# Routing a mixture of experts back to its tokens: row scatters in place of row gathers in a decoder block on one core

## The chip, the cores and the metric

The kernel runs on one core of a Trainium2 chip. The metric is the device time of one execution in microseconds (us). The engines are TensorE (PE in profiles; its weight loads are PEld), VectorE (DVE), ScalarE (ACT), GpSimd (POOL) and SyncE (SP, which here only issues transfers). Each works through its own queue in order; they meet at semaphores. Transfers (DMAs) issued by SP and ACT, and those issued by GpSimd, share sixteen DMA engines.

## The reference

One decoder block on x of 8 sequences x 256 tokens x 256 features, all in float32. Three steps, each followed by a LayerNorm over the sum with its input: causal self-attention with 16 heads; three rounds of slot attention over a context of 120 rows with a GRU cell; and a mixture of experts. The last step is where the change lies:

```python
router_probs = softmax(x @ gate_w + gate_b)              # 8 experts
expert_values, expert_indices = top_k(router_probs, k=2)
expert_values = expert_values / (sum(expert_values) + 1e-09)
all_outputs = gelu(x @ ew1[e] + eb1[e]) @ ew2[e] + eb2[e]  # 256 -> 1024 -> 256
moe_out = sum over the two chosen experts of value * output
return x + mlp(x, shared weights) + moe_out
```

Only the two chosen experts of a token matter to its result.

## The kernel before

There are NT = 2048 tokens in NBLK = 4 blocks of 512; a block is four groups of 128 tokens, a token to a partition. `X[i]` holds block i with tokens on the partitions, `XT[i]` the same with features on the partitions.

Attention comes first, then the slot attention as twelve phases (three rounds of four blocks). At the start of the second stage `zeros` fills two tables in DRAM through SP: `xd` and `yd`, each 16,640 rows of 256 numbers. A table has a region of 2048 rows for each expert, and a tail of rows that stay zero.

Routing of block i: `route_rest(i)` makes the probabilities, the two one-hot choices `hot1` and `hot2` and the weights `wt1` and `wt2`. In `best`, `first` is the rank (8 for expert 0, down to 1 for expert 7) of the chosen expert. `place(i)` counts, for each token, which row of its expert's region it gets, and writes the row numbers into `slots[0]` and `slots[1]`. Then GpSimd scatters the block to `xd`: eight indirect DMAs (line 892), four groups times two choices, 128 rows each. The 32 scatters of all blocks are declared independent of one another (`declare_no_dep`), so that none waits for another's landing. place(0) comes in the last phase of the second stage, place(1), (2) and (3) between units of the shared MLP.

`tables()` works out, from the counts of each expert, which expert and which rows each of the 23 tiles gets: 16 pair tiles of 256 rows and 7 single tiles of 128 rows, enough for every possible routing. Rows that no token filled are zero. SP reads the tile's expert and first row into registers (`tei`, `tri`).

For each tile: `tile_fetch` loads its rows of `xd` (line 1114), waiting by hand-written dependencies for all 32 scatters; `tile_weights` and `tile_weights2` load the expert's weights (2 MB a tile); `tile_turn` transposes the rows on TensorE (line 1147); `tile_up` (line 1044, `ph_t`) and `tile_down` (line 1058, `pf_t`) are the two matrix products with gelu on ScalarE between them (line 1053). `tile_down` adds the bias into `yo` and stores it through SP to the tile's rows of `yd` (line 1162). The tiles are pipelined: the up product of a tile comes ahead of the down product of the one before.

The shared MLP is cut into eight units u of 256 tokens with the same two products (`ph_s`, `pf_s`). Units 0 to 3 come before the tiles, among the routing; units 4 to 7 come after them, in the tail. `Z[i]` collects the result of block i.

The tail: `fetch_back(i)` gathers, for each group and choice, the 128 rows of `yd` by `slots` with an indirect DMA of GpSimd (line 1172), 32 in all, into 16 buffers `y`. `take_back(i)` adds them to `Z[i]` with their weights (line 1186, eight VectorE operations a block). `finish` applies the LayerNorm and stores the output (line 1190). The order is written out:

```python
    shared_up(4)
    fetch_back(0)
    shared_up(5)
    fetch_back(1)
    take_back(0)
    parts(4)
    take_back(1)
    shared_up(6)
    ...
    for i in range(2):
        finish(i, 0, NSUB)
    fetch_back(2)
```

The order on TensorE and ScalarE is that of the program throughout; in the tail also that on VectorE and GpSimd. Everything else, SP always among it, is put in order by the planner of the framework, which also inserts the semaphores. It knows a dependency through DRAM only by the table: an indirect access may touch any row of it.

Of the kernel before, what the change touches and what calls it, by code (L numbers as in the profile page):

```python
# [18 lines left out]
NT = B * S  # L19
# [27 lines left out]

SHARED_FIRST = 4

NY = 16  # L50
LN_EPS = 1e-5
RMS_EPS = 1e-6
ATT_EPS = 1e-6
# [8 lines left out]
def decoder_kernel(  # L62
# [44 lines left out]
            nc.scalar.copy(dst, src)  # L107


    X = [act.tile([P, NSUB, D], F32, tag=f"X{i}", name=f"X{i}") for i in range(NBLK)]  # L110
    XT = [act.tile([P, DC, BLK], F32, tag=f"XT{i}", name=f"XT{i}") for i in range(NBLK)]

    def load_x(i):
# [407 lines left out]
    b2p = stage2.enter_context(tc.tile_pool(name="b2", bufs=2))  # L521

    shared = load_shared()
    zeros = b1.tile([P, D], F32, name="zeros")
# [288 lines left out]
    def route_rest(i):  # L813

        shape = [P, NSUB, NE]

        def t(name):
            return fr2.tile(shape, F32, tag=name, name=f"{name}_{i}")

        def s(name):  # L820
            return fr2.tile([P, NSUB], F32, tag=name, name=f"{name}_{i}")

        def wide(a):
            return a.unsqueeze(2).to_broadcast(shape)
# [17 lines left out]
        def best(src, k, hot):  # L842
            top, first = s(f"top{k}"), s(f"first{k}")
# [11 lines left out]
        top2 = best(rest, 2, hot2[:, blk, :])  # L855
# [11 lines left out]
    puts = []  # L867

    def place(i):

        blk = ts(i, NSUB)
        shape = [P, NSUB, NE]
        pc = bank(f"place_{i}")[:, 0 : NSUB * NE]
        flat = [a[:, blk, :].rearrange("p n e -> p (n e)") for a in (cur, before)]
        nc.tensor.matmul(pc, upper, flat[0], start=True, stop=False)
        nc.tensor.matmul(pc, ones, flat[1], start=False, stop=True)
        row = fr2.tile(shape, F32, tag="row", name=f"row_{i}")
        tt(
            row,
            pc.rearrange("p (n e) -> p n e", e=NE),  # L880
            first_row[:, 0:NE].unsqueeze(1).to_broadcast(shape),
            ALU.add,
        )
        for j, hot in enumerate((hot1, hot2)):
            tt(hot[:, blk, :], hot[:, blk, :], row, ALU.mult)
            at_row = fr2.tile([P, NSUB], F32, tag=f"at_row{j}", name=f"at_row{j}_{i}")
            nc.vector.tensor_reduce(at_row, hot[:, blk, :], AX.X, ALU.add)
            nc.vector.tensor_copy(slots[j][:, blk], at_row)
        for n in range(NSUB):
            for slot in slots:  # L890
                g = i * NSUB + n
                put = nc.gpsimd.indirect_dma_start(
                    out=xd[:, :],
                    out_offset=bass.IndirectOffsetOnAxis(ap=slot[:, g : g + 1], axis=0),
                    in_=X[i][:, n, :],
                    in_offset=None,
                )
                if puts:
                    tc.declare_no_dep(put.ins, group="puts", reason="other rows")
                tc.add_to_no_dep_group("puts", put.ins)  # L900
                puts.append(put)

    def tables():

# [194 lines left out]
        tt(z, z, po, ALU.add)  # L1099
        yield  # L1100

    TI = {}

    def groups(t):
        return 2 if t < NPAIRT else 1
# [4 lines left out]
    def tile_fetch(t):  # L1110

        row = nc.sync.value_load(tri[0:1, t : t + 1], min_val=0, max_val=ROWS - RT)
        xg = f2.tile([P, 2, D], F32, tag="xg", name=f"xg_{t}", bufs=4)[:, 0 : groups(t), :]
        load = nc.sync.dma_start(xg, rows_of(xd, row, t))
        for put in puts:
            tc.add_manual_dep(
                load.ins,
                put.ins.name,
                mybir.DependencyInfo(mybir.DependencyClass.Sync, mybir.DependencyReason.DATA),
                reason="rows of the table",  # L1120
            )
        TI[t] = [row, xg]

    def tile_weights(t):

# [7 lines left out]
        TI[t] += [w1_sb, w2_sb, bt, b2t, e]  # L1133

    def tile_weights2(t):

        row, xgT, w1_sb, w2_sb, bt, b2t, e = TI[t]
        nc.sync.dma_start(w2_sb, ew2[ds(e, 1), :, :].rearrange("e (c p) d -> p (e c) d", p=P))
        nc.sync.dma_start(b2t, b2[ds(e, 1), :].to_broadcast([P, D]))

    def tile_turn(t):
# [8 lines left out]
        TI[t][1] = xgT  # L1150

    def tile_up(t):
        row, xgT, w1_sb, w2_sb, bt, b2t, e = TI[t]
        HT["t", t] = up(w1_sb, bt, xgT, f"t{t}")

    def tile_down(t):
        row, xgT, w1_sb, w2_sb, bt, b2t, e = TI.pop(t)
        n = groups(t)
        po = down(w2_sb, HT.pop(("t", t)), f"t{t}", groups=n)
        yo = f2.tile([P, 2, D], F32, tag="yo", name=f"yo_{t}")[:, 0:n, :]  # L1160
        tt(yo, po[:, 0:n, :], b2t.unsqueeze(1).to_broadcast([P, n, D]), ALU.add)
        nc.sync.dma_start(rows_of(yd, row, t), yo)

    Y = {}

    def fetch_back(i):

        for n in range(NSUB):
            for j, slot in enumerate(slots):
                g = i * NSUB + n  # L1170
                y = f2.tile([P, D], F32, tag="y", name=f"y_{g}_{j}", bufs=NY)
                nc.gpsimd.indirect_dma_start(  # L1172
                    out=y,
                    out_offset=None,
                    in_=yd[:, :],
                    in_offset=bass.IndirectOffsetOnAxis(ap=slot[:, g : g + 1], axis=0),
                )
                Y[g, j] = y

    def take_back(i):  # L1180

        for n in range(NSUB):
            g = i * NSUB + n
            for j, wt in enumerate((wt1, wt2)):
                z = Z[i][:, n, :]
                nc.vector.scalar_tensor_tensor(z, Y.pop((g, j)), wt[:, g : g + 1], z, ALU.mult, ALU.add)  # L1186

    def finish(i, n0, n1):
        layernorm(Z[i][:, n0:n1, :])
# [154 lines left out]
```

## Time and profile before

| | |
|---|---|
| median of 9 runs | 1095.49 us (1094.92 to 1097.65) |
| the profiled execution | 1097.89 us, of which the span of instructions is 1096.2 |
| TensorE busy | 1040.5 us, 95% of the span |
| ScalarE, VectorE, GpSimd busy | 475.5, 469.6, 237.6 us |
| mean granted TensorE clock | 0.982 of full speed |
| moved by DMA | 144.24 MB, mean 132 GB/s |
| GpSimd's gathers, line 1172 | 32, 946 ns median each |
| GpSimd's scatters, line 892 | 32, 960 ns median each |
| expert weights | 46 loads of 1 MB, 5.6 us to landing (median) |

A row of a timeline or of the chain gives the start in us from the span's beginning, the duration in us, the engine, the line of the kernel, the operation, what it writes and reads, and how often. In brackets stands how long the engine had been idle and whose event ended that. "issue" is time in which an engine waited for nothing that the profile shows; "remote" or "an unknown queue" is a wait whose releaser the profile can't name. "SPq" is SP's own queue of instructions. A row of stretches gives, for each engine, busy us and the number of instructions in it, the granted clock, the share of time that the DMA engines were busy, and GB/s.

### The profile page before, as it was taken

Reading aid. Unit: us, or ns where it says so; the run is one execution under the profiler, and the core shown is the slowest. Engines: PE = TensorE matmul, PEld = TensorE weight load, DVE = VectorE, ACT = ScalarE, POOL = GpSimd, SP = SyncE. Lnnn points to the kernel's source line nnn. Section 1 sums busy time; section 2 is a strip of 40 time slices with the busy share of each in tenths; the row PEclk is TensorE's granted clock in tenths of the full one; section 3 lists DMA queues with packets and bytes.
Section 4 is the critical chain, followed back from the end, with each engine's and each line's share of the span. In section 5 each row is a group of like instructions: output and inputs, shape, how many; then the busy total and the mean of one; then the engine's idle time right before and its main releaser. Section 6 shows DMA issues by size and latency. Waiting matters only on the chain. (4 is left out here: it accounts for less than half of the span.)

```text
span 1096.2 us, 13674 instructions
## 1 busy us (share of the span) xinstructions
PE 1040.5 (95%) x4686; PEld 720.4 (66%) x4686; DVE 469.6 (43%) x1394; ACT 475.5 (43%) x1140; POOL 237.6 (22%) x264
## 2 busy tenths in 40 slices
PE   8999999999888999999999999699999999999867
PEld 4444555555445755555565668588888888888756
DVE  3666666666676542434443677400011011110137
ACT  3567776666676024555555443123222222222213
POOL 2333423532234221121211023500000000000550
PEclk9999999999999999999999998999999999999969
DMA  9644433333344499940000011246676767663231
GB/s 326 105 78 82 87 70 61 73 73 72 70 90 89 150 348 348 349 145 0 1 1 1 0 39 39 78 154 219 205 243 208 232 202 250 213 211 110 84 92 64
DMA packets 195492, 144.24 MB, mean 132 GB/s; under 512 B 107551, under 2 KB 185951, under 8 KB 195423
## 3 DMA queue, kind: packets, MB, share of 16 engines
q1 hardware_dynamic: 191263, 132.88, 42.7%
q0 software_dynamic: 3072, 8.39, 2.4%
q10 hardware_dynamic: 1088, 2.10, 0.5%
q8 instruction: 37, 0.61, 0.2%
q14 instruction: 32, 0.26, 0.1%
HBM read 72.70 MB, written 45.48 MB: 108 GB/s over the span
## 5 line engine op out<-in xcount | busy, mean ns | idle before, releaser
L1053 ACT ACTIVATE hT_t<-ph_t,bt 128x256 f32<-128x256 f32 (+1 forms) x184 | 71.1, 437 | 202.7 <-issue 154.6
L363 POOL TENSOR_TENSOR sc<-sc,sums 128x256 f32<-128x256 f32 (+1 forms) x128 | 105.2, 843 | 213.2 <-DVE sums L360 213.2
L348 ACT ACTIVATE sc<-sc,nmax 128x128 f32<-128x128 f32 (+1 forms) x256 | 113.3, 444 | 73.8 <-DVE nmax L335 73.8
L1044 PE MATMUL ph_t<-xgT,w 128*128 128x256 f32 (+1 forms) x736 | 140.3, 348 | 0.8 <-ACT hT_t L1053 0.8
L1058 PE MATMUL pf_t<-w,hT_t 128*128 128x256 f32 x624 | 138.3, 379 | 0.0
L739 PE MATMUL gate<-XT,whh_sb 128*128 128x512 f32 x288 | 133.8, 593 | 0.0
L1044 PEld LDWEIGHTS ph_t<-xgT,w 128*128 128x128 f32 x736 | 123.8, 190 | 15.0 <-ACT hT_t L1053 1.0
L1058 PEld LDWEIGHTS pf_t<-w,hT_t 128*128 128x128 f32 x624 | 116.9, 190 | 15.0
L1172 POOL DMA_INDIRECT y<-yd,slot x32 | 30.7, 959 | 323.8 <-PE ph_s L1044 309.2
L335 DVE CUSTOM_DVE_ANT_0 sc<-pp,mask 128x128 f32<-128x128 f32 (+1 forms) x256 | 76.3, 354 | 54.2 <-PE pp L323 53.3
L377 ACT COPY planes<-sc 128x1536 uint16<-128x1536 uint16 x64 | 93.2, 1457 | 8.5 <-POOL sc L363 8.5
L1044 PE MATMUL ph_s<-XT,sh 128*128 128x256 f32 x256 | 66.5, 415 | 20.8 <-issue 11.3
L739 PEld LDWEIGHTS gate<-XT,whh_sb 128*128 128x128 f32 x288 | 54.2, 189 | 48.5 <-issue 46.2
L399 PEld LDWEIGHTS po<-pT,v 128*64 128x64 f32 x512 | 33.2, 137 | 68.3 <-issue 25.5
L1044 PEld LDWEIGHTS ph_s<-XT,sh 128*128 128x128 f32 x256 | 52.9, 209 | 33.0 <-issue 14.6
L399 PE MATMUL po<-pT,v 128*64 128x256 f32 (+1 forms) x512 | 56.4, 340 | 19.1 <-DVE pT L385 13.9
L748 PEld LDWEIGHTS gate<-at,G 120*128 120x128 f32 x288 | 54.5, 189 | 29.9 <-issue 23.3
L748 PE MATMUL gate<-at,G 120*128 120x256 f32 x288 | 72.1, 379 | 0.4 <-DVE at L598 0.4
L1149 DVE COPY xgT<-xg 128x512 f32<-128x512 f32 (+1 forms) x23 | 14.0, 610 | 131.7 <-PE xg L1147 131.7
L385 DVE COPY pT<-turned 128x1536 uint16<-128x1536 uint16 x64 | 69.3, 1082 | 0.0
L598 DVE TENSOR_TENSOR yo<-pf_t,b2t 128x512 f32<-128x512 f32 (+1 forms) x23 | 14.0, 611 | 127.9 <-PE pf_t L1058 127.9
L1053 ACT ACTIVATE hT_s<-ph_s,vec_sb 128x256 f32<-128x256 f32 x64 | 26.7, 470 | 90.5 <-PE ph_s L1044 45.5
(208 smaller groups left out, 1479.9 us busy)
## 6 DMA issues: line engine op xcount, KB each, us to landing
w<-in_ew_dram SPq DMA_DIRECT2D x46, 1024.0 KB, 5.6
xd<-zeros SPq DMA_DIRECT2D x1, 16640.0 KB, 51.2
yd<-zeros SPq DMA_DIRECT2D x1, 16640.0 KB, 99.4
xg<-xd SPq DMA_DIRECT2D x16, 256.0 KB, 5.4
yd<-yo SPq DMA_DIRECT2D x16, 256.0 KB, 5.7
b2t<-in_b_dram SPq DMA_DIRECT2D x23, 128.0 KB, 5.4
sh<-in_sh_w_dram SPq DMA_DIRECT2D x2, 1024.0 KB, 6.9
X<-in_x_dram SPq DMA_DIRECT2D x3, 512.0 KB, 11.6
```

The source lines that it names most:

```text
L335: nc.vector.tensor_tensor_reduce(out=sc[:, h, seg[t]], in0=pp[h][:, seg[t]], in1=mask[:, seg[t]], scale=-(HD**-0.5), scalar=3.0e38, op0=AL ...
L348: nc.scalar.activation(sc[:, h, seg[t]], sc[:, h, seg[t]], AF.Exp, scale=-1.0, bias=nmax[:, t, h : h + 1], accum_out=sums[:, t, h : h + 1],)
L363: nc.gpsimd.tensor_tensor(sc[:, :, seg[t]], sc[:, :, seg[t]], sums[:, t, :].unsqueeze(2).to_broadcast([P, 2, w]), ALU.mult,)
L377: nc.scalar.copy(planes, sc.rearrange("p h c -> p (h c)").bitcast(U16).rearrange("p (n w) -> p w n", w=2))
L385: nc.vector.tensor_copy(pT.rearrange("p h c -> p (h c)").bitcast(U16).rearrange("p (n w) -> p w n", w=2), turned.rearrange("p (w c) q -> p ...
L399: nc.tensor.matmul(po[ts(h, HD), q0:S], V[i][:, 2 * bi + c, ts(2 * pr + h, HD)], pT[:, h, 0:S] if c == 0 else pT[:, h, S:384], start=c == ...
L739: nc.tensor.matmul(pg[:, oc, :], whh_sb[:, dc, o], XT[i][:, dc, :], start=dc == 0, stop=not given and dc == DC - 1,)
L748: nc.tensor.matmul(pg[:, oc, ts(bi, S)], G[:, BPB * i + bi, o], AT_[p][:, bi, :], start=not hidden, stop=not hidden or bi == BPB - 1,)
L1044: nc.tensor.matmul(ph[:, a, 0:w], w1_sb[:, dc, ts(c, P)], rhs[:, dc, :], start=dc == 0, stop=dc == DC - 1,)
L1053: nc.scalar.activation(hT[:, c, 0:w], ph[:, a, 0:w], AF.Gelu_apprx_tanh, bias=bias[:, c : c + 1])
L1058: nc.tensor.matmul(po, hT[:, c, ts(a, P)], w2_sb[:, c, :], start=c == 0, stop=c == FC - 1)
L1172: nc.gpsimd.indirect_dma_start(out=y, out_offset=None, in_=yd[:, :], in_offset=bass.IndirectOffsetOnAxis(ap=slot[:, g : g + 1], axis=0),)
```

## The change

The tables change their meaning. A row of `xd` becomes 272 numbers: the token's 256 features, then twice its number plus two (an iota written once at the start), then the rank of its first expert. `X[i]` is now a view of a wider tile `XW[i]`. `yd` is no longer laid out by expert but by token: two rows for each token, first the output of its second choice, then that of its first; two spare rows at the front take what padding rows write. So `yd` needs no zeros.

When a tile has been fetched, one VectorE operation works out for each of its rows where the output goes: twice the token's number plus two, plus one if the tile's expert is the token's first. `tile_down` then scatters `yo` to these rows, one indirect DMA of GpSimd for each group of 128 rows: 39 for the 23 tiles. `fetch_back` becomes a plain load of 1 MB a block through SP, into two buffers.

The declaration that the scatters of `place` are independent is dropped, and with it the hand-written dependencies of the fetches: each scatter now waits for the one before it, to `xd` and to `yd` alike, and the fetches wait for the last. Ahead of the first tile the order changes too: tile 0's weights are issued ahead of the fetches, three tiles are fetched at once, and the turn of the first tile stands between the halves of unit 3's down product in place of ahead of both.

```diff
-    X = [act.tile([P, NSUB, D], F32, tag=f"X{i}", name=f"X{i}") for i in range(NBLK)]
+    XW = [act.tile([P, NSUB, DW], F32, tag=f"X{i}", name=f"X{i}") for i in range(NBLK)]
+    X = [t[:, :, 0:D] for t in XW]
...
-    xd = tc.dram_tile([ROWS, D], F32, name="xd")
-    yd = tc.dram_tile([ROWS, D], F32, name="yd")
+    xd = tc.dram_tile([ROWS, DW], F32, name="xd")
+    yd = tc.dram_tile([2 * (NT + 1), D], F32, name="yd")
+    for i in range(NBLK):
+        nc.gpsimd.memset(XW[i][:, :, D:DW], 0.0)
+        nc.gpsimd.iota(XW[i][:, :, D], pattern=[[2 * P, NSUB]], base=2 * (i * BLK + 1), ...
...
-    for table in (xd, yd):
-        nc.sync.dma_start(
-            table.rearrange("(p r) d -> p r d", p=P), zeros.unsqueeze(1).to_broadcast([P, ROWS // P, D])
-        )
+    nc.sync.dma_start(
+        xd.rearrange("(p r) d -> p r d", p=P), zeros.unsqueeze(1).to_broadcast([P, ROWS // P, DW])
+    )
...
-        top1 = best(pb, 1, hot1[:, blk, :])
+        top1 = best(pb, 1, hot1[:, blk, :], XW[i][:, :, D + 1])
...
-                put = nc.gpsimd.indirect_dma_start(
+                nc.gpsimd.indirect_dma_start(
                     out=xd[:, :],
                     out_offset=bass.IndirectOffsetOnAxis(ap=slot[:, g : g + 1], axis=0),
-                    in_=X[i][:, n, :],
+                    in_=XW[i][:, n, :],
                     in_offset=None,
                 )
-                if puts:
-                    tc.declare_no_dep(put.ins, group="puts", reason="other rows")
-                tc.add_to_no_dep_group("puts", put.ins)
-                puts.append(put)
...
+        nc.vector.tensor_scalar(tile_rank, te, -1.0, float(NE), ALU.mult, ALU.add)
...
+        to = f2.tile([P, 2], I32, tag="to", name=f"to_{t}", bufs=3)
+        nc.vector.scalar_tensor_tensor(
+            to[:, 0:n], xg[:, :, D + 1], tile_rank[:, t : t + 1], xg[:, :, D], ALU.is_equal, ALU.add
+        )
...
-        nc.sync.dma_start(rows_of(yd, row, t), yo)
+        for k in range(n):
+            nc.gpsimd.indirect_dma_start(
+                out=yd[:, :],
+                out_offset=bass.IndirectOffsetOnAxis(ap=to[:, k : k + 1], axis=0),
+                in_=yo[:, k, :],
+                in_offset=None,
+            )
...
-        for n in range(NSUB):
-            for j, slot in enumerate(slots):
-                g = i * NSUB + n
-                y = f2.tile([P, D], F32, tag="y", name=f"y_{g}_{j}", bufs=NY)
-                nc.gpsimd.indirect_dma_start(
...
+        y = f2.tile([P, NSUB, 2, D], F32, tag="y", name=f"y_{i}")
+        nc.sync.dma_start(
+            y, yd[2 * (i * BLK + 1) : 2 * ((i + 1) * BLK + 1), :].rearrange("(n p j) d -> p n j d", p=P, j=2)
+        )
...
-    for t in TILES[:2]:
-        tile_fetch(t)
     tile_weights(TILES[0])
     tile_weights2(TILES[0])
+    for t in TILES[:3]:
+        tile_fetch(t)
     for u in range(2, SHARED_FIRST):
         shared_up(u)
+        next(part[u])
         if u == SHARED_FIRST - 1:
-            tile_fetch(TILES[2])
             tile_weights(TILES[1])
             tile_turn(TILES[0])
-        parts(u)
+        next(part[u])
```

More of the change, by code (lines that the diff above doesn't have):

```diff
@@ L48 @@
 SHARED_FIRST = 4
-NY = 16
+DW = D + 16
 LN_EPS = 1e-5
@@ L150, in decoder_kernel @@
     )
-    xd = tc.dram_tile([ROWS, D], F32, name="xd")
-    yd = tc.dram_tile([ROWS, D], F32, name="yd")
+    xd = tc.dram_tile([ROWS, DW], F32, name="xd")
+    yd = tc.dram_tile([2 * (NT + 1), D], F32, name="yd")
+    for i in range(NBLK):
+        nc.gpsimd.memset(XW[i][:, :, D:DW], 0.0)
+        nc.gpsimd.iota(
+            XW[i][:, :, D],
+            pattern=[[2 * P, NSUB]],
+            base=2 * (i * BLK + 1),
+            channel_multiplier=2,
+            allow_small_or_imprecise_dtypes=True,
+        )
     for h in range(2):
@@ L523, in decoder_kernel @@
     shared = load_shared()
-    zeros = b1.tile([P, D], F32, name="zeros")
+    zeros = b1.tile([P, DW], F32, name="zeros")
     nc.gpsimd.memset(zeros, 0.0)
-    for table in (xd, yd):
-        nc.sync.dma_start(
-            table.rearrange("(p r) d -> p r d", p=P), zeros.unsqueeze(1).to_broadcast([P, ROWS // P, D])
-        )
+    nc.sync.dma_start(
+        xd.rearrange("(p r) d -> p r d", p=P), zeros.unsqueeze(1).to_broadcast([P, ROWS // P, DW])
+    )
     fh = ctx.enter_context(tc.tile_pool(name="fh", bufs=2, side="right"))
@@ L840, in route_rest, with best @@
         rankb = rank.unsqueeze(1).to_broadcast(shape)
-        def best(src, k, hot):
-            top, first = s(f"top{k}"), s(f"first{k}")
+        def best(src, k, hot, first):
+            top = s(f"top{k}")
             nc.vector.tensor_reduce(top, src, AX.X, ALU.max)
@@ L851, in route_rest @@
         blk = ts(i, NSUB)
-        top1 = best(pb, 1, hot1[:, blk, :])
+        top1 = best(pb, 1, hot1[:, blk, :], XW[i][:, :, D + 1])
         rest = t("rest")
         nc.vector.scalar_tensor_tensor(rest, hot1[:, blk, :], -2.0, pb, ALU.mult, ALU.add)
-        top2 = best(rest, 2, hot2[:, blk, :])
+        top2 = best(rest, 2, hot2[:, blk, :], s("first"))
         den = s("den")
@@ L864, in route_rest @@
             tt(before[:, g + 1, :], before[:, g, :], cur[:, g, :], ALU.add)
-    puts = []
     def place(i):
@@ L891, in place @@
                 g = i * NSUB + n
-                put = nc.gpsimd.indirect_dma_start(
+                nc.gpsimd.indirect_dma_start(
                     out=xd[:, :],
                     out_offset=bass.IndirectOffsetOnAxis(ap=slot[:, g : g + 1], axis=0),
-                    in_=X[i][:, n, :],
+                    in_=XW[i][:, n, :],
                     in_offset=None,
                 )
-                if puts:
-                    tc.declare_no_dep(put.ins, group="puts", reason="other rows")
-                tc.add_to_no_dep_group("puts", put.ins)
-                puts.append(put)
+    tile_rank = fr.tile([P, NTILE], F32, name="tile_rank")
     def tables():
@@ L1100, in shared_down @@
         yield
-    TI = {}
+    TI, TW = {}, {}
     def groups(t):
@@ L1112, in tile_fetch @@
         row = nc.sync.value_load(tri[0:1, t : t + 1], min_val=0, max_val=ROWS - RT)
[L1113 to L1122, printed above, removed]
+        xg = f2.tile([P, 2, DW], F32, tag="xg", name=f"xg_{t}", bufs=4)[:, 0 : groups(t), :]
+        nc.sync.dma_start(xg, rows_of(xd, row, t))
+        TI[t] = [None, xg]
     def tile_weights(t):
@@ L1132, in tile_weights @@
         nc.sync.dma_start(bt, vecs[:, ds(e * FC, FC)])
-        TI[t] += [w1_sb, w2_sb, bt, b2t, e]
+        TW[t] = [w1_sb, w2_sb, bt, b2t, e]
     def tile_weights2(t):
-        row, xgT, w1_sb, w2_sb, bt, b2t, e = TI[t]
+        w1_sb, w2_sb, bt, b2t, e = TW[t]
         nc.sync.dma_start(w2_sb, ew2[ds(e, 1), :, :].rearrange("e (c p) d -> p (e c) d", p=P))
@@ L1149, in tile_turn @@
         nc.vector.tensor_copy(xgT, pt)
-        TI[t][1] = xgT
+        to = f2.tile([P, 2], I32, tag="to", name=f"to_{t}", bufs=3)
+        nc.vector.scalar_tensor_tensor(
+            to[:, 0:n], xg[:, :, D + 1], tile_rank[:, t : t + 1], xg[:, :, D], ALU.is_equal, ALU.add
+        )
+        TI[t][0:2] = to, xgT
     def tile_up(t):
-        row, xgT, w1_sb, w2_sb, bt, b2t, e = TI[t]
+        (to, xgT), (w1_sb, w2_sb, bt, b2t, e) = TI[t], TW[t]
         HT["t", t] = up(w1_sb, bt, xgT, f"t{t}")
     def tile_down(t):
-        row, xgT, w1_sb, w2_sb, bt, b2t, e = TI.pop(t)
+        (to, xgT), (w1_sb, w2_sb, bt, b2t, e) = TI.pop(t), TW.pop(t)
         n = groups(t)
@@ L1161, in tile_down @@
         tt(yo, po[:, 0:n, :], b2t.unsqueeze(1).to_broadcast([P, n, D]), ALU.add)
-        nc.sync.dma_start(rows_of(yd, row, t), yo)
+        for k in range(n):
[5 more added lines that the diff above has]
+            )
     Y = {}
     def fetch_back(i):
-        for n in range(NSUB):
-            for j, slot in enumerate(slots):
-                g = i * NSUB + n
-                y = f2.tile([P, D], F32, tag="y", name=f"y_{g}_{j}", bufs=NY)
-                nc.gpsimd.indirect_dma_start(
[L1173 to L1178, printed above, removed]
+        y = f2.tile([P, NSUB, 2, D], F32, tag="y", name=f"y_{i}")
+        nc.sync.dma_start(
+            y, yd[2 * (i * BLK + 1) : 2 * ((i + 1) * BLK + 1), :].rearrange("(n p j) d -> p n j d", p=P, j=2)
+        )
+        Y[i] = y
     def take_back(i):
@@ L1183, in take_back @@
             g = i * NSUB + n
-            for j, wt in enumerate((wt1, wt2)):
+            for j, wt in enumerate((wt2, wt1)):
                 z = Z[i][:, n, :]
-                nc.vector.scalar_tensor_tensor(z, Y.pop((g, j)), wt[:, g : g + 1], z, ALU.mult, ALU.add)
+                nc.vector.scalar_tensor_tensor(z, Y[i][:, n, j, :], wt[:, g : g + 1], z, ALU.mult, ALU.add)
     def finish(i, n0, n1):
```

## The prediction

> **What bounds the kernel now.** I read the slices of the page first, then the chain that ended last, then the waits, stretches and timeline of the two places where TensorE's row falls below nine. TensorE has work 95% of the span; from 744 to 1016 us it is busy 271.4 of 272 us and nothing can be gained. Two places remain: the approach to the first expert tile and the tail. In the slices (one digit a slice of 27.4 us, tenths busy, then the granted clock):
>
> ```profile
> PE   8999999999888999999999999699999999999867
> PEclk9999999999999999999999998999999999999969
> ```
>
> The "6" at slice 26 is the approach, the last three digits are the tail. The chain through the tail (start, us, what):
>
> ```profile
> 1016.79 13.55 PE ph_s L1044 x56
> 1030.37 0.84 ACT hT_s L1053 x2
> 1031.21 5.47 another core or an unknown queue
> 1036.70 0.85 ACT hT_s L1053 x2
> ...
> 1038.08 0.38 PE ph_s L1044
> 1038.45 1.72 issue
> 1040.17 0.38 PE ph_s L1044
> ...
> 1054.17 7.85 PE ph_s L1044 x23
> ```
>
> TensorE issues one matmul every 1.4 to 2.1 us here, where 0.22 is normal, though nothing it needs is missing. The waits from 1015 us on say the same of the other engines (total, times, longest):
>
> ```profile
> ACT hT_s L1053 <- remote: 22.5, 2, 17.0
> DVE Z L598 <- remote: 21.7, 1, 21.7
> ```
>
> Three engines crawl together, and the timeline has one thing running all the while: GpSimd's gathers of line 1172, 24 back to back every 1.25 us from 1020.5 to 1050.3 us. They run untroubled for eight or nine, then the crawl sets in and ends some 4 us after the last. The same appears with the scatters of line 892: sixteen back to back from 691.1 to 711.4 us, and in the stretches (busy of PE, PEld, DVE, ACT, POOL; clock; DMA share; GB/s)
>
> ```profile
> 690.00:700.00 10.00, 10.00 (x50) 8.89 (x50) 4.22 (x30) 0.46 (x2) 6.76 (x8) 1.00 0.23 81
> 700.00:710.00 10.00, 3.05 (x13) 2.02 (x12) 4.33 (x25) 0.84 (x2) 7.84 (x8) 0.91 0.29 105
> ```
>
> the first eight cost TensorE nothing, the second eight most of its time. The DMA engines are under a third busy, so it isn't bandwidth. What exactly is blocked the trace does not name; I price only what it shows. That it is no artefact of the profiler follows from the times: the profiled execution took 1097.89 us (span 1096.2 and 1.7 around it), the median of the plain runs is 1095.49. A crawl of some 28 us (17.6 in the tail, about 10 in the approach, both below) that only profiled runs had would have put them much further apart. So profile and runs differ by 2.4 us, and I make the sum on the profile and move the median by it.
>
> **Removed: the gathers (tail).** From 1016.79 to TensorE's last matmul at 1089.64 are 72.85 us. The work is four shared up and four shared down units of 6.91 us each (the chain's ph_t and pf_t pieces have this length at full clock): 55.3. The difference, 17.6 us, is crawl and the half clock after it (0.65 in 1037.5 to 1062). With no GpSimd DMA in the tail it goes: -17.6. What is late next? The plain loads. The last tile's yo ends at 1017.5 us; two scatters one after another at 2.8 us (below) end at 1023.1; a 1 MB load takes 5.6 us to land (the expert weights' row), so block 0 is there at 1029 and block 1 about 3 us later (1 MB at the page's 348 GB/s). Block 0 was folded in by 1032.65 before; eight folds of 0.48 us give the same now. ScalarE needs LayerNorm 0 only after the gelus of unit 6, at about 1046 (1016.8 plus four units and a table load). Covered. Blocks 2 and 3 wait for a y buffer (two), free by 1033 and 1042, needed at about 1054 and 1063 (1072.1 and 1080.5 now, less 17.6). That holds if SP issues the last load when its buffer is free. If it stands behind block 2's output store (issued about 1063), it lands at 1069, 6 us late.
>
> **Added: scatters of line 892 one by one.** Without the declaration each waits for the landing of the one before. GpSimd's rows now (start, us, [idle before]):
>
> ```profile
> 643.06 1.17 POOL L892 DMA_INDIRECT xd<-X,slot  x1 [32.12 <-DVE slot L888]
> 665.61 0.95 POOL L892 DMA_INDIRECT xd<-X,slot  x1 [12.45 <-DVE at_row L887]
> 691.11 0.95 POOL L892 DMA_INDIRECT xd<-X,slot  x1 [14.98 <-DVE slot L888]
> ```
>
> Place 0, 1 and 2 start there; place 3 follows 2 directly. The cadence today is 0.96 + 0.30 = 1.26 us. The price of a wait is not in the trace for a scatter. Nearest row: the first gather starts at 1020.53, and VectorE starts on its data at 1023.33, 2.80 us later; same engine, same 128 rows. Lower end: the 128 KB output store lands 1.7 us after issue, plus 0.30: 2.0. Upper end: generation 0.96 plus 2.8, the landing of the 512 KB store: 3.76. I take 2.8; rows of 1088 instead of 1024 bytes add 6% to a data phase well under 1 us.
>
> By the Trainium skill, "DMA: Bandwidth & Descriptors", Anatomy of one DMA, a GpSimd DMA takes about 2.0 us plus bytes at 436 GB/s, an estimate of 2.3 us here; the approach would then cost 1.5 us and not 6.5 (place 2 starts at 691), the sum would be -16.1.
>
> Place 0 fills 643.1 to 665.5, so place 1 still starts at 665.6 and ends at 688.0. Place 2 is ready at 691 or, without the crawl of 672 to 678, some us sooner, so I run on without a gap: 665.6 + 24 x 2.8 = 732.8 us. Behind the waiting scatters GpSimd has nothing else queued (its timeline from 643 to 1020 holds only these). On SP the fetches wait for the last; expert weights of tile 0 now stand ahead of them, and what may queue behind, tile 1's first weights, is needed a whole tile later. First rows: 0.6 us of waking and issue plus 2.7 landing (the shortest fetch): 736.1. TensorE, freed of the crawl (7.86 us idle at 703.9 and the half clock around it), is at the turn of the first tile at 717 to 722 (728.95 now, 10 to 15 of crawl less, half a unit more) and waits. After the turn (0.44) only half a shared unit is left before tile 0, 3.46 us, and a resuming TensorE runs at half clock: 2.8 us, as after the tail's crawl (23 matmuls in 7.85 us). Tile 0 starts at T + 3.3 + 0.44 + 3.46 + 2.8 = T + 10.0 = 742.8, against
>
> ```profile
> 736.30 4.05 PE L1044 MATMUL ph_t<-xgT,w 128*128 128x256 f32 x18
> ```
>
> now: +6.5. The crawl's gain here is already inside this number: the idle time comes back as a wait. In general +(24c - 60.7) for a cadence c; at 2.0 place 2 readies at 691 and the chain is 691 + 32 + 10: -3.
>
> Against the change speaks the Trainium skill, "SBUF — State Buffer", SBUF: two separate sides: VectorE can lock GpSimd out of writing descriptors during fp32 copies in SBUF. A copy of 0.69 us per scatter would add 17 us to the chain and turn the sum to +5. The row that decides: the 32 scatters took 954/960/1546 ns (min/median/max) with VectorE busy 7.5 of 12.4 us beside place 1, so the lock, if any, cost 0.6 us once. I take zero.
>
> **Added: 39 scatters of tile rows** (16 tiles of two groups, 7 of one) in place of 23 stores on SP. Two pair tiles and a single take 35.9 us for five groups, 7.2 us a scatter; at 2.8, or even 0.96 + 5.7 (the store's landing beside weight loads) = 6.7, they keep up. If one took over 7.2, yo's two buffers would fill, VectorE and TensorE wait, 39 us for each us above. Crawl: isolated scatters show none (eight in a row left TensorE at 10.00 of 10). Many padding rows go to one row of yd; no row prices that, the slack is 4.4 us a scatter. Zero.
>
> **Edits with one answer.** The zero fill of yd (16.6 MB in 378 to 480 us) goes, xd's grows 6%; TensorE is at nine throughout and the next user of xd comes at 643: 0. The 0.19 us VectorE operation a tile, table operations and wider tiles: VectorE is busy 26.5 of 272 us in the loop: 0. Memsets and iotas at the start lie on GpSimd after the identity, its next work being at 12.95 us: 0, at worst 1 if x's load waited for them. Sum: -17.6 + 6.5 = -11.1; profile 1086.8, median 1084.4.
>
> **Rivals.** (1) The scatter chain is longer: from c = 3.26 the approach costs more than the tail gives; at 3.76 it is +29.5 - 17.6 = +12, 1107. For it: writes to DRAM may land later than gathers; against: the small stores' 1.7 us. Slower. (2) SP issues block 3 late: 6.5 us less gain, -4.6, 1091. (3) Short cadence, 2.0 to 2.4: -16 to -21, 1075 to 1079. (4) The crawl is not the gathers' doing, or scatters spread out bring it back: no tail gain, +6.5, 1102. Against: it starts and ends with the bursts, twice.
>
> **How the numbers follow.** Forecast 45%, (3) 15%, (2) 13%, (1) 20%, (4) 7%. No change is what the measurement can't tell, 0.2% or 2.2 us; it lies between (2) and (1), 5%. Faster 0.71, same 0.05, slower 0.24. The range takes in (3) nearly whole, (2), (4) and (1) up to c = 3.6: 1076 to 1104; the forecast's own is 1079 to 1090.
>
> **What would show it.** Scatters of 892 some 2.8 us apart, ending near 733; TensorE idle 14 to 19 us before the first turn, tile 0 near 743; the loop unchanged at 35.9 us per three tiles; no gap in the tail, about 62 us from last tile to end where 79.4 are now. Wrong if the cadence leaves 2.0 to 3.3, the tail keeps "remote" waits, or the loop shows TensorE waiting for VectorE.

## The result, and the profile after

The kernel after the change takes 1115.01 us (median of 10 runs, 1113.55 to 1118.87). The kernel before, run beside it, took 1095.57 (31 runs), a ratio of 1.0179, 95% interval [1.0165, 1.0193]. The change is slower by 1.8%; forecast were 1084.4 us, faster, and the time lies above the range. The profiled execution of after took 1115.45 us, its span 1113.7, against 1097.89 and 1096.2. One run of the later copy of after, 1543.15 us at a granted clock of 0.652, was slow and is left out of its ratio.

Three cuts of the span say where the time went. The last column is an unchanged copy of each kernel in a later comparison, to which the experiments lead.

| us | before | after | difference | the same pair, run later |
|---|---|---|---|---|
| approach: start to tile 0's up product | 736.3 | 747.3 | +11.0 | 720.9, 746.4: +25.5 |
| loop: from there to the end of the last tile | 280.3 | 304.7 | +24.4 | 280.3, 304.8: +24.5 |
| tail: the rest | 79.6 | 61.7 | -17.9 | 62.1, 61.8: -0.3 |
| span | 1096.2 | 1113.7 | +17.5 | 1063.3, 1113.0: +49.7 |

The slices of after (one digit for 27.8 us):

```profile
PE   8999999999888999999999999739899899999997
PEclk9999999999999999999999999969999999999999
```

The tail is whole now, the approach has a deep notch with the clock down, and eights have come into the loop, where before there were only nines.

**Approach.** The stretches of after (busy of PE, PEld, DVE, ACT, POOL; clock; DMA share; GB/s) and GpSimd's timeline (start, us, what, and in brackets the idle time before it):

```profile
700.00:710.00 10.00, 10.00 (x48) 8.79 (x47) 1.77 (x10) 1.44 (x4) 1.92 (x2) 1.00 0.73 230
718.00:741.40 23.40, 0.01 (x1) 0.04 (x1) 0.04 (x1) 0.00 (x0) 6.73 (x7) 0.57 0.21 72
```

```profile
700.99 0.96 POOL L899 DMA_INDIRECT xd<-X,slot  x1 [1.77 <-DMA xd<-X,slot]
703.68 0.96 POOL L899 DMA_INDIRECT xd<-X,slot  x1 [1.73 <-DMA xd<-X,slot]
710.35 0.96 POOL L899 DMA_INDIRECT xd<-X,slot  x1 [5.71 <-DMA xd<-X,slot]
713.05 0.96 POOL L899 DMA_INDIRECT xd<-X,slot  x1 [1.74 <-DMA xd<-X,slot]
```

The crawl of 700 to 710 us (the three engines slowed beside an unbroken burst of GpSimd's transfers) is gone: 10.00 of 10 us busy, where before had 3.05. The scatters wait for each other's landing, 2.7 us from start to start, once 6.67. TensorE then stands idle for 23 us, until the chain is through and the first rows are fetched, and resumes slowly, with 5.16 us for sixteen matmuls that take 3.62 elsewhere:

```profile
741.39 1.09 PE L1147 MATMUL xg<-ident,xg 128*128 128x128 f32 x4 [23.46 <-DMA xg<-xd]
742.28 5.16 PE L1065 MATMUL pf_s<-sh,hT_s 128*128 128x256 f32 x16
747.28 7.07 PE L1051 MATMUL ph_t<-xgT,w 128*128 128x256 f32 x32
```

**Loop.** Two lines from the waits of after (total, times, longest):

```profile
DVE to L1152 <- DMA yd<-yo,to: 145.0, 20, 12.0
PE ph_t L1051 <- issue: 16.2, 6, 2.8
```

VectorE, busy for a tenth of the loop, waits 145 us in the small operation that works out the row numbers `to`, and what releases it is the landing of a scatter. One of the six places where TensorE notices, from the timelines of the three engines:

```profile
788.40 0.96 POOL L1168 DMA_INDIRECT yd<-yo,to  x1 [5.49 <-DMA yd<-yo,to]
793.63 0.22 DVE L1152 SCALAR_TENSOR_TENSOR to<-xg,tile_rank 128x2 int32<-128x2 f32 x1 [11.95 <-DMA yd<-yo,to]
793.76 0.68 DVE L1149 COPY xgT<-xg 128x512 f32<-128x512 f32 x1
794.55 7.14 PE L1051 MATMUL ph_t<-xgT,w 128*128 128x256 f32 x32 [2.81 <-issue]
```

`to` has three buffers. The operation of line 1152 writes a buffer whose old numbers belong to a scatter that is still on its way, so it waits for that scatter, which started at 788.40 and landed at 793.6. (Whether the scatter still reads its numbers so late the trace does not show; it shows that the wait ends with the landing.) Behind it in VectorE's queue stands the copy of the turned rows, `xgT`, which ran as soon as the queue was free; TensorE started on it 0.8 us later, after 2.81 us of idling. The turn of these rows had begun at 787.69. The six gaps make 16.2 us, and four of the six pieces behind them take 8.83 us in place of 7.07, another 7.0 (the granted clock is 0.80 in the piece from 833.44, 1.00 in the one shown): 23.2 of the loop's 24.4.

**Tail.** TensorE's part of it, and the stretch:

```profile
1051.99 13.98 PE L1051 MATMUL ph_s<-XT,sh 128*128 128x256 f32 x64
...
1093.43 13.98 PE L1065 MATMUL pf_s<-sh,hT_s 128*128 128x256 f32 x64
```

```profile
1051.99:1113.70 61.71, 55.42 (x257) 48.45 (x255) 34.35 (x104) 20.30 (x47) 1.92 (x2) 0.98 0.30 107
```

55.42 us of matmuls without a gap, no wait put down to "remote". The first load of `yd` is issued at 1058.25; block 0 is folded in from 1064.0.

### The profile page after: what moved, and what is told of

It is laid out like the page before. It is cut to its first block, busy times and chain, and to the rows that moved or that the text cites. A ratio compares the mean times of both kernels' runs of the same rounds, so it can differ in the third digit from the quotient of the medians.

```text
span 1113.7 us, 13632 instructions
## 1 busy us (share of the span) xinstructions
PE 1040.8 (93%) x4686; PEld 721.1 (65%) x4686; DVE 471.6 (42%) x1418; ACT 476.4 (43%) x1140; POOL 245.9 (22%) x279
## 5 line engine op out<-in xcount | busy, mean ns | idle before, releaser
L1051 PE MATMUL ph_t<-xgT,w 128*128 128x256 f32 (+1 forms) x736 | 147.5, 360 | 17.0 <-issue 16.2
L1051 PEld LDWEIGHTS ph_t<-xgT,w 128*128 128x128 f32 x736 | 128.1, 197 | 35.2 <-issue 18.4
L1168 POOL DMA_INDIRECT yd<-yo,to x39 | 37.5, 962 | 282.3 <-DVE yo L608 208.5
L1152 DVE SCALAR_TENSOR_TENSOR to<-xg,tile_rank 128x2 int32<-128x2 f32 (+1 forms) x23 | 5.1, 221 | 178.7 <-DMA yd<-yo,to 145.0
L410 PEld LDWEIGHTS po<-pT,v 128*64 128x64 f32 x512 | 33.2, 137 | 68.0 <-issue 25.5
L758 PEld LDWEIGHTS gate<-at,G 120*128 120x128 f32 x288 | 54.5, 189 | 29.9 <-issue 23.2
L309 PE MATMUL pq<-XT,wq_sb 128*128 128x512 f32 x128 | 64.5, 627 | 0.2 <-DVE XT L105 0.2
L309 PE MATMUL pq<-XT,wk_sb 128*128 128x512 f32 x128 | 63.3, 617 | 0.0
L319 PE MATMUL pv<-wv_sb,XT 128*128 128x512 f32 x128 | 59.4, 594 | 0.0
L1065 PE MATMUL pf_s<-sh,hT_s 128*128 128x256 f32 x256 | 58.6, 387 | 0.0
## 6 DMA issues: line engine op xcount, KB each, us to landing
xd<-zeros SPq DMA_DIRECT2D x1, 17680.0 KB, 54.6
```

The lines of the kernel that those rows point to most:

```text
L309: nc.tensor.matmul(pq, w[:, dc, ts(pr, P)], XT[i][:, dc, :], start=dc == 0, stop=dc == DC - 1)
L410: nc.tensor.matmul(po[ts(h, HD), q0:S], V[i][:, 2 * bi + c, ts(2 * pr + h, HD)], pT[:, h, 0:S] if c == 0 else pT[:, h, S:384], start=c == ...
L758: nc.tensor.matmul(pg[:, oc, ts(bi, S)], G[:, BPB * i + bi, o], AT_[p][:, bi, :], start=not hidden, stop=not hidden or bi == BPB - 1,)
L1051: nc.tensor.matmul(ph[:, a, 0:w], w1_sb[:, dc, ts(c, P)], rhs[:, dc, :], start=dc == 0, stop=dc == DC - 1,)
L1065: nc.tensor.matmul(po, hT[:, c, ts(a, P)], w2_sb[:, c, :], start=c == 0, stop=c == FC - 1)
```

## The experiments: the loop

The theories, by the letters that the expectations use. **A**: `to`'s three buffers hold VectorE up, and the `xgT` copy behind it. **B**: the two buffers of `yo` do. **C**: a scatter lands late because weights are loading, not because it writes scattered rows. **E**: at the approach the order of the scatters costs the time, and without it the crawl comes back. **D** is C's rival. F, G and H mean different things from one comparison to the next; each expectation says what.

**Deeper row numbers**

```diff
-        to = f2.tile([P, 2], I32, tag="to", name=f"to_{t}", bufs=3)
+        to = f2.tile([P, 2], I32, tag="to", name=f"to_{t}", bufs=8)
```

> The changed kernel with eight buffers for the row numbers `to` in place of three. Theory A (the wait is for a buffer of `to`: the operation that writes it stands on VectorE until the scatters that still read the old numbers have landed, and the copy of the next tile's transposed rows stands behind it): the loop from the first tile's up product to the end of the last down product goes from 304.7 us back to about 280.5, the total from 1115 to about 1091. Theory B (scatters of 5 to 6 us one after another cannot keep up with the tiles, so yo's two buffers fill): no change, 1113 to 1117.

1091.13 us, ratio to before 0.9951 [0.9933, 0.9969]; loop 280.3 us, as before the change. TensorE's issue waits in the loop are gone, while GpSimd's scatters wait for landings no less than they did (after's 73.8 us are 102.5 here). The line of after, then of this run:

```profile
L1168 POOL DMA_INDIRECT yd<-yo,to x39 | 37.5, 962 | 282.3 <-DVE yo L608 208.5 <-DMA yd<-yo,to 73.8
L1168 POOL DMA_INDIRECT yd<-yo,to x39 | 37.4, 959 | 258.3 <-DVE yo L608 155.8 <-DMA yd<-yo,to 102.5
```

So the 24 us went into too few buffers of a few numbers each, and not into the rate of the scatters.

**Deeper outputs**: `yo` with four buffers in place of two, `to` as in after.

> The changed kernel with four buffers for yo in place of two; `to` keeps three. Theory A: no change, 1113 to 1117, loop 304 to 306 us. Theory B: the loop loses its gaps, about 1091.

1112.84 us, ratio 1.0155 [1.0133, 1.0178]; loop 302.1, the six waits still there (15.2 us). B falls.

**Two tiles' weights only**: the expert weights are loaded for the first two tiles alone and used by all others, so the experts' outputs are those of other experts.

```diff
+        if len(FIRST) == 2:
+            TW[t] = FIRST[TILES.index(t) % 2]
+            return
...
+        if t not in TILES[:2]:
+            return
```

> The changed kernel, with the expert weights loaded for the first two tiles only; all later tiles use those two sets, so the expert outputs are another function and 42 MB of loads are left out. Theory C (a scatter lands late in the loop because 1 MB weight loads share its DMA engines): scatters 2.7 us apart as at the tail, not 5 to 6; a pair's two scatters have landed within about 6 us, and `to` waits no longer hold up the copy: loop about 281 us, total about 1091. Rival D (late because the rows written are scattered and many padding rows go to one row): scatters stay 5 to 6 us apart, total 1113 to 1117.

1091.75 us, ratio 0.9959 [0.9947, 0.9971]; loop 280.4, with three buffers of `to`. The pairs of scatters:

```profile
803.37 0.96 POOL L1174 DMA_INDIRECT yd<-yo,to  x1 [13.34 <-DVE yo L608]
806.04 0.96 POOL L1174 DMA_INDIRECT yd<-yo,to  x1 [1.71 <-DMA yd<-yo,to]
```

2.67 us apart, where after has 5.3 to 6.5 in the loop where a scatter waits for the landing before it and weights are loading. From issue to landing a scatter takes 2.4 us here in the median, 5.0 in after. The same rows are written, padding rows among them: C holds. A scatter is the slower for 2 MB of weights a tile beside it, and three buffers suffice when it isn't: `to` still waits 67.2 us in all, but TensorE never waits for it.

**Row numbers later in the program**: line 1152 moved into `tile_down`, three buffers.

> The changed kernel with three buffers for `to` as it is, but the operation that writes it moved from the turn of the tile to just ahead of its scatters. Theory A (what costs is the place of this operation on VectorE, where it waits for landings ahead of the next tile's copy): its buffer has been free for two tiles, nothing waits, loop about 281 us, total about 1091. Rival (slow landings hold up the loop whatever the place): 1105 to 1117.

A miss that tells nothing: 1114.58 us, ratio 1.0164 [1.0137, 1.0192]. The planner put the operation in the same place of VectorE's queue (147.3 us of waits for landings). So once more, held there by a dependency:

```diff
+        add = nc.vector.tensor_tensor(yo, po[:, 0:n, :], ...)
+        to = f2.tile([P, 2], I32, tag="to", name=f"to_{t}", bufs=3)
+        where = nc.vector.scalar_tensor_tensor(to[:, 0:n], ...)
+        tc.add_manual_dep(where.ins, add.ins.name, ..., reason="after the sum")
```

> The changed kernel with three buffers for `to`, the operation that writes it tied behind the sum into yo by a dependency, since moving it in the program left VectorE's order as it was. Theory A: its buffer was last read three tiles ago, nothing waits, the copy of the next rows is never behind it: loop 280 to 283 us, total 1089 to 1093. Rival (the slow landings themselves hold up the loop, through yo or the queue of GpSimd): 1105 to 1117.

Loop 280.3 us and 1088.94, with three buffers: it is the place of the waiting operation ahead of `xgT` that costs, as much as the number of buffers. Its ratio of 1.024 [1.021, 1.0269] does not fit, since the kernel before took 1065.22 us in that comparison, 30 less than in any other so far. That is taken up below.

## The experiments: approach and tail

**Scatters into xd independent again**, with after's other parts: the declaration and the fetches' dependencies put back.

> The changed kernel with the declaration that the scatters into xd are independent put back, and with it the hand-written waits of the fetches; nothing else. Theory E (one-by-one landing sets the start of the first tile, but it also spares the crawl of the back-to-back bursts): scatters 1.26 us apart, the last near 710 us, the crawl of TensorE between 700 and 712 comes back, the first tile starts at about 733 to 737 us and not 747.3: total about 1102 to 1105. Rival F (the crawl belonged to the gathers or to the order before the first tile): no crawl, first tile at about 722 to 726 us, total about 1091.

1101.07 us, ratio 1.0057 [1.0038, 1.0076]. Scatters 1.26 us apart, tile 0 at 732.99 (14 us sooner than after), the crawl back:

```profile
707.73 3.78 PE L1057 MATMUL ph_s<-XT,sh 128*128 128x256 f32 x8 [7.19 <-ACT hT_s L1066]
```

**Both mends** (deep `to`, independent scatters):

> The changed kernel with both cures: eight buffers for `to`, and the scatters into xd declared independent. Theory (the two losses are separate terms): tile 0 starts at about 733 us as with free scatters, the loop takes 280.5 us, the tail 61.7: total about 1076 to 1079, 1.7% below the kernel before. Rival (the two share a cause, so that the gains do not add): 1085 or more.

1076.94 us, ratio 0.9818 [0.9796, 0.984]: the terms add. TensorE is busy 14.86 of the 25 us from 693 to 718, so the crawl is all there.

**Two in flight**: as that, but each scatter into `xd` waits for the one two before it.

> As the kernel with both cures, but each scatter into xd waits for the one two before it, so that at most two are under way. Expected 1.4 us apart on the average, the last near 711 us. Theory G (the crawl comes from many GpSimd transfers under way or queued): no crawl, TensorE without the 7 to 8 us gap, tile 0 at about 723 to 727 us, total 1067 to 1072. Theory H (it comes from GpSimd making descriptors nearly without pause): the crawl stays, tile 0 at 733 to 736, total 1076 to 1080.

1066.15 us, ratio 0.9723 [0.9702, 0.9744], as G expected to within a microsecond. Timeline and stretch of 693 to 718 us:

```profile
718.95 0.63 PE L1167 MATMUL xg<-ident,xg 128*128 128x128 f32 x4 [1.91 <-DMA xg<-xd]
719.41 3.62 PE L1078 MATMUL pf_s<-sh,hT_s 128*128 128x256 f32 x16
722.87 7.07 PE L1064 MATMUL ph_t<-xgT,w 128*128 128x256 f32 x32
```

```profile
693.00:718.00 25.00, 24.04 (x112) 20.82 (x110) 7.86 (x50) 6.71 (x16) 11.72 (x12) 1.00 0.51 171
```

No crawl, nearly no wait, tile 0 at 722.87. Within a burst most scatters start 1.26 to 1.5 us apart, a few up to 4.8.

**Work moved into the wait**: deep `to`, and two of the tail's shared units ahead of the tiles.

```diff
-SHARED_FIRST = 4
+SHARED_FIRST = 6
...
```

> The changed kernel with eight buffers for `to`, scatters one by one, and shared units 4 and 5 moved from the tail to ahead of the first tile. Theory (TensorE is idle 23.5 us there only because the chain of 32 landings is longer than its work): the idle shrinks to about 9.7 us, tile 0 still starts at 747 us; the tail loses 13.8 us of TensorE work, but the folding and the LayerNorms of four blocks (about 33 us of VectorE after the first load, and 9 us of end) do not fit beside it any more, so about 7 of the 13.8 come back: total about 1082 to 1086. Rival (the first tile waits for something else than the landings): tile 0 starts 10 us or more later than 747.

1086.24 us, ratio 0.9907 [0.9882, 0.9933]. Tile 0 stays at 746.4 and the wait is filled, but the tail shrinks from 61.7 to 54.6 us only, not by the 27.6 us of matmuls taken out (four pieces of 6.91; the expectation counted two): TensorE waits there once for 18.4 us, for ScalarE's gelu.

**The kernel before with its gathers two at a time**, and **a fill between scatters** (both mends and a GpSimd fill of 128x256 ahead of each scatter into `xd`), beside the pinned numbers:

```diff
+                if len(gets) > 1:
+                    tc.add_manual_dep(get.ins, gets[-2].ins.name, ..., reason="two in flight")
```

```diff
+                nc.gpsimd.memset(pause, 0.0)
                 put = nc.gpsimd.indirect_dma_start(
```

> The kernel BEFORE, with one edit: each gather of the tail waits for the one two before it. Scatters, tables and loop as before. Theory (the tail's 17.6 us were the crawl beside unbroken bursts of GpSimd transfers, and waiting for landings spares it whatever the transfers are): gathers about 1.4 us apart, no gap of TensorE in the tail, tail about 62 to 65 us, total 1078 to 1082. Rival (the tail gained because loads took the place of gathers): tail 77 to 82 us, total 1093 to 1099.

> As the kernel with both cures (eight buffers for `to`, scatters into xd independent), with a GpSimd memset of 128x256 ahead of every scatter into xd, so that they come some 1.8 to 2 us apart without waiting for a landing. Theory H (the crawl comes from GpSimd making descriptors without pause): no crawl, tile 0 at about 723 to 729, total 1066 to 1072. Theory G (only waiting for landings, so fewer transfers under way, spares it): the crawl stays, total 1076 or more.

1078.11 us, ratio 1.0121 [1.0104, 1.0139], and 1066.26, 1.0011 [0.9998, 1.0024]. Neither told anything of the crawl: the gathers' version still has free scatters at the approach, 32 of them, and TensorE was busy 25.00 of 25 us beside them. The kernel before took 1065 us there. Was the crawl a matter of the single chip? Before and after were profiled again, beside each other:

> The kernel before, unchanged, profiled once more. In the last comparison (gathers two, pause) it took 1065.2 us, 30 us less than the 1096 of all comparisons before that, and no run of that comparison showed the crawl of the instruction queues, not even the free bursts of 32 scatters. Theory F (the crawl is a property of the single chip, or of how the program came to lie on it, and the bursts only bring it out): either the time is 1094 to 1098 us and the profile shows TensorE gaps of 7 us and more beside the scatters at 690 to 712 us and waits put down to 'remote', or it is 1063 to 1067 us, and then the profile shows TensorE busy for over 24.5 of the 25 us of 693 to 718, tile 0's up matmuls start at 721 to 725, and the tail after the last tile is 61 to 66 us in place of 79. Theory G (the crawl was always there and the 30 us came from elsewhere, the granted clock above all): at a time of 1063 to 1067 us the profile still shows the gaps, and the granted clock in the loop is higher than 0.99 where it was lower before.

> The kernel after, unchanged, beside the kernel before on the same chip. It shows no crawl on a chip that has one, so theory F expects the same 1111 to 1117 us whichever chip this is: a ratio of 1.015 to 1.020 where the kernel before takes 1096, and of 1.043 to 1.050 where it takes 1065. Theory G expects it to be 25 to 30 us faster too wherever the kernel before is: 1085 to 1090 us and a ratio of 1.016 to 1.022 on either chip.

This chip had no crawl either. Before took 1064.94 us (1065.32 in the 19 runs beside it), and after 1.0456 [1.0421, 1.0491] times as long. The stretch of the first profile of before, then the same stretch here, a piece of the timeline here, and one of after's:

```profile
693.00:718.00 25.00, 16.31 (x71) 13.54 (x70) 9.28 (x55) 3.35 (x8) 14.10 (x15) 0.86 0.26 90
```

```profile
693.00:718.00 25.00, 25.00 (x119) 22.01 (x119) 8.53 (x50) 6.70 (x16) 10.36 (x11) 1.00 0.48 164
```

```profile
713.56 0.60 PE L1147 MATMUL xg<-ident,xg 128*128 128x128 f32 x4
713.99 7.07 PE L1058 MATMUL pf_s<-sh,hT_s 128*128 128x256 f32 x32
720.90 7.07 PE L1044 MATMUL ph_t<-xgT,w 128*128 128x256 f32 x32
...
1001.24 13.98 PE L1044 MATMUL ph_s<-XT,sh 128*128 128x256 f32 x64
```

```profile
740.16 1.09 PE L1147 MATMUL xg<-ident,xg 128*128 128x128 f32 x4 [23.39 <-DMA xg<-xd]
```

The same instructions in the same order, GpSimd's bursts 1.26 us apart as ever, and TensorE isn't disturbed at all: tile 0 at 720.90, a tail of 62.1 us (1063.3 less 1001.24). After is the same as ever, 23 us of idling included. What F forecast came, and G falls: the loop takes 280.3 us at a granted clock of 1.00 in both profiles of before, and the 33 us by which their spans differ (1096.2 and 1063.3) are 15.4 us at the approach and 17.5 in the tail. Of the 15.4, 3.0 are there before the first scatter starts (643.06 against 640.08), so some 12.4 belong to the scatters' crawl. The other two kernels were run there once more as well:

> The kernel before with each of the tail's 32 gathers waiting for the one two before it. On the chip without the crawl this cost 13 us (1078.1 against 1065.2), since gathers at 1.6 us apart feed the tail more slowly than free ones at 1.27. On a chip with the crawl, theory F expects the crawl in the tail to be gone and the one at the approach to stay: gathers some 1.6 us apart, no wait put down to 'remote' after 1010 us, a tail of 72 to 79 us, and a time of 1086 to 1096 us beside 1096. If the waits for 'remote' stay in the tail, gathers two at a time crawl as well, and it is not the unbroken burst that brings it out. On a chip without it the 1078 repeats.

> Deep tile numbers, scatters into xd independent, and a fill of 128x256 on GpSimd ahead of each of those 32 scatters (1.46 us apart in place of 1.27). Without the crawl it was level with the kernel before (1066.3 against 1065.2), as two chains would be. On a chip with the crawl: if a short break between two descriptor writings is enough, there are no gaps at 690 to 712 us and the time is 1064 to 1068 us beside 1096, a ratio of 0.970 to 0.974, as for two chains; if what counts is the number of scatters in flight, the gap of 7 to 9 us at 707 to 709 us is back and the time is 1074 to 1080 us, as for the version without the fill.

1077.41 us, ratio 1.01 [1.0078, 1.0121], and 1064.83, ratio 0.9997 [0.9985, 1.0009], as on the other chip without a crawl.

A last comparison fell on a chip with the crawl, the kernel before at 1100.33 us. **The kernel before with fills** ahead of its scatters and its gathers, and nothing of the change, came with the same two again:

> The kernel before with a fill of 128x256 on GpSimd ahead of each of the 32 scatters into xd and of each of the 32 gathers, and nothing of the change: scatters and gathers 1.46 us apart in place of 1.27 and 1.25. On a chip without the crawl (kernel before at 1065): the approach has slack, and the gathers end 32 x 0.2 = 6.5 us later, of which VectorE's chain in the tail takes up some: 1065 to 1072 us. On a chip with the crawl (kernel before at 1096): if a break between two descriptor writings is enough, both crawls are gone and the time is the same 1065 to 1072 us, a ratio of 0.971 to 0.979, and no wait is put down to 'remote'; if the breaks do not help, it is 1094 to 1104 us.

> As the gathers two at a time before; it can only tell on a chip where the kernel before takes 1096 us. There theory F expects a crawl at the approach as before (a TensorE gap of 7 us or more at 700 to 712 us) and none in the tail: 1086 to 1096 us, no wait for 'remote' after 1010 us. If the waits for 'remote' stay in the tail, it is not the unbroken burst that brings the crawl out. On a chip without the crawl 1075 to 1079 us once more.

> As the fill between the scatters before; it can only tell on a chip where the kernel before takes 1096 us. There, if a break of 0.5 us between two descriptor writings is enough, 1064 to 1068 us and no gaps at 690 to 712 us; if the number in flight counts, 1074 to 1080 us with the gap back. On a chip without the crawl 1064 to 1067 us once more.

1073.36 us, ratio 0.9755 [0.9738, 0.9771]; 1095.81, ratio 0.9963 [0.9953, 0.9974]; 1066.5, ratio 0.9699 [0.9683, 0.9715]. The version with gathers two at a time, first the approach and then the tail:

```profile
714.67 3.78 PE L1044 MATMUL ph_s<-XT,sh 128*128 128x256 f32 x8 [9.35 <-issue]
...
1061.01 5.41 PE L1044 MATMUL ph_s<-XT,sh 128*128 128x256 f32 x16 [2.31 <-ACT hT_s L1053]
```

Free scatters crawl on this chip, gathers held to two in flight don't: the one gap left in the tail is 2.31 us, 2.35 where nothing crawls, and the tail is 74.4 us on both kinds of chip. It is longer than 62 since the gathers come 1.6 us apart and more: the last starts 59 us after the tail's first matmul, 43 where they are free and nothing crawls. Now the fills. The stretch of 693 to 718 us beside free scatters (the version with gathers two at a time), then in the kernel before with fills:

```profile
693.00:718.00 25.00, 14.77 (x63) 12.20 (x62) 9.49 (x55) 2.52 (x6) 14.96 (x16) 0.83 0.24 85
693.00:718.00 25.00, 24.15 (x113) 20.95 (x112) 9.01 (x55) 5.76 (x14) 17.87 (x28) 1.00 0.29 97
```

TensorE is busy 24.15 of 25 us, against 14.77 on the same chip. A wait of 8.9 us put down to "remote" is left on ScalarE and costs TensorE under 1 us. With the fills its tail is 66.1 us, and its time lies just above the 1065 to 1072 us expected. So a fill in the burst is enough, and 27 of the 34 us that the best version wins on this chip are had without the change. Whether the break counts or the lower rate (1.46 us in place of 1.26) no run separates.

## Why the prediction was wrong, point by point

**The loop: "Two pair tiles and a single take 35.9 us for five groups … they keep up … Zero", and "The 0.19 us VectorE operation a tile … 0."** The step that failed is the second of these zeros, and it cost 24.4 us. The first had the rate right: at 5.3 to 6.5 us beside the weights (6.7 was the upper figure) the scatters do fit into 7.2. But a buffer is held for the latency, not the rate. I followed only `yo`; the numbers `to` are held longer, from the turn of their tile until its last scatter has landed (those written at 793.63 went out with the scatters of 821.35 and 827.14), and the operation that refills them stands in VectorE's queue ahead of work that TensorE needs at once. It was priced by its 0.19 us and by VectorE's low load, as if it could not wait. The sign named for this, TensorE waiting for VectorE in the loop, came, though the profile puts the waits down to "issue". More buffers, a later place in the queue, or faster landings each took the 24 us away.

**Approach, +6.5: measured +11.0.** The mechanism was right, with TensorE idle and tile 0 late; the chain was mis-sized: it ended at 738.4, not at 732.8, while the way from there to tile 0's up product took 8.9 us, not 10.0. 2.8 us a scatter was the ordinary case (median 2.73), but the chain took 95.9 us from 642.5 to 738.4, 3.0 a scatter: several steps of 3.2 to 3.9 us from start to start, and one of 6.67 while tile 0's weights, issued at 702.3 to 704.0, were loading. The landing beside weight loads stood in the prediction for the tiles and was not applied to the approach, where the change itself had moved weights ahead of the fetches. By the Trainium skill, "DMA: Bandwidth & Descriptors", Anatomy of one DMA, about 2.0 us are fixed and the rest goes by bytes, an estimate of 2.3 here; the 2.4 us from issue to landing in quiet are near that, the 5.0 in the median beside 1 MB loads are not, and the measurement decides.

**VectorE locking GpSimd out, zero: right but for a little.** What the Trainium skill, "SBUF — State Buffer", SBUF: two separate sides, would make of it, by the prediction's estimate 17 us in the chain, does not show: a scatter of line 899 is busy 1.02 us in the mean, 0.96 in the median, and 27 of the 31 waits in the chain end with a landing. Two scatters of place 1 took 1.29 and 2.07 us; a lock there can have cost 1.4. The prediction's 7.5 of 12.4 us was read from 668.3 us on; beside all eight scatters of place 1, from 665.6 to 678.0, VectorE was busy 10.1 of 12.4.

**Tail, -17.6: right in size (-17.9), not in kind.** The crawl goes when the gathers go, the loads of `yd` are covered, and rivals 2 and 4 did not happen. But the gain is not always there. In the five comparisons of the experiments, each on a chip of its own, before took 1096 to 1100 us in three and 1065 in two. Where nothing crawls, the tail gives 0.3 us and the approach costs 25.5. That the crawl is no artefact of the profiler was right; that it belongs to the kernel was an assumption I did not see that I made.

**The sum.** -17.6 + 6.5 = -11.1 against a measured -17.9 + 11.0 + 24.4 = +17.5. Rival 1 had the sign, at the approach; the price fell in the loop. Without a crawl it is -0.3 + 25.5 + 24.5 = +49.7.

What stays open: why the crawl is there in some comparisons and not in others, and what is blocked. Different programs with free bursts agreed within each comparison; but each chip was used for one comparison only, so that the chip itself, where things come to lie in its memory, and the time of the runs can't be told apart. Shown are the conditions: unbroken bursts of GpSimd's transfers, on some of the chips, and that a fill or a landing waited for between them takes nearly all of it away.

The best version is the change with deep row numbers and broken-up scatters: 0.9723 (two in flight) and 0.9699 (fill) of the time before on two chips with the crawl, 0.9997 and 1.0011 (both fill) on two without it. Where nothing crawls, then, even the best version wins nothing.

## What to carry to other kernels

When a store becomes a transfer that reads its addresses from a buffer, count the buffers of the addresses by the landing time, as you do those of the data; and look what stands behind their refill in its engine's queue. An "issue" or "remote" wait that no instruction explains may not belong to the kernel: run the kernel on another chip before a change is priced by it, and try a break in the burst before a rewrite.

## What the runs showed of the hardware

- A scatter of 128 rows of 1 KB by GpSimd lands so that the next one waiting for it starts some 2.7 us later in quiet (2.67 in after's tail, 2.73 in the median at its approach), and 5.3 to 6.5 us later beside loads of 1 MB (after's loop). From issue to landing it is 2.4 us at the least, and 5.0 in the median of after's tile scatters.
- Bursts of GpSimd's transfers at 1.25 to 1.27 us slow down the instruction issue of TensorE, ScalarE and VectorE on three of the five chips: some 12 us at the approach and 17.5 in the tail of this kernel. At 1.46 us, with a fill between, under 1 us of TensorE's time is left of the first and some 4 us of tail, of which the later gathers are a part.
- Waiting for the landing of the transfer two before costs scatters into `xd` little (mostly 1.26 to 1.5 us apart), and spreads gathers from 1.25 to 1.6, so that the same rule lengthened the tail by 12 us where nothing crawled.
